# Span attention later in the batch, shorter, with its sums on ScalarE: one change to a perceiver block on one Trainium2 core

## The chip, the core and the metric

The kernel runs on one core of one Trainium2 chip. The core has a matrix engine (TensorE, PE in profiles; PEld is its loading of weights), a vector engine (VectorE, DVE), an activation engine (ScalarE, ACT), a general one (GpSimd, POOL), a queue engine that starts most transfers here (SyncE, SP), and DMA engines. Every engine works through its own list of instructions in order and waits for the others by semaphores. TensorE writes to PSUM, which VectorE and ScalarE read; GpSimd works on SBUF alone here. The metric is the device time of one execution in microseconds (us).

## The reference

Thirty-two sequences of 64 latent rows of width 256 go through three blocks, each with a layer norm before it and a residual addition after it. All values are float32.

```python
x = x + xattn(layernorm(x), ctx, ctx, mask)  # 16 heads of 16; ctx has 1601 rows per sequence
x = x + span_attn(layernorm(x))
x = x + ffn(layernorm(x))                    # gated dense part, and two of eight experts per row
```

The span attention is the part of most interest here. For each head it computes two numbers per row and a distribution over the 64 positions:

```python
span = heads(h @ W_span.T, 2);  value = heads(h @ W_val.T, 16)
mean = sigmoid(span[..., 0]) * 64
soft = softplus(span[..., 1])
scores = -soft * (pos - mean) ** 2
out = softmax(scores) @ value
return merge(out) @ W_out.T
```

## The kernel before

**Cross attention, in halves of a batch.** The loop over `halves` (L696) runs over the 32 sequences ("batches" in the code) and, in each, over c = 0 and 1, eight heads at a time. The 1601 context rows lie in 13 blocks of 124, and these in four groups (`GROUPS`: four blocks, then three times three). One pass of the loop is half n. It has four stretches, g = 0 to 3, numbered 4n + g, and in each the code issues for every engine, in this order: the scores of the *next* half for group g (`scores`, TensorE, into four PSUM banks, and VectorE takes them out with the mask added, L504); projections of the next batch (`project_keys`, `project_values`, TensorE, and ScalarE takes them out, L465 and L482); a subtraction of the maxima of *this* half for one of four pairs of heads (`less_maxima`, L556, on GpSimd in the loop); then the steps that the agenda holds for this stretch (`run`); and one exponential of a pair (`exponentials`, L561, ScalarE).

The maxima over the blocks are gathered in `mrun`, a PSUM tile: `first_maxima` (L517, ScalarE) copies block 0 into it at the end of g = 0, and VectorE takes the further blocks in (`maximum`, L525) between the evictions and after those of g = 3, where the last one writes `mx`. In g = 0 of the next half TensorE turns it (`turned_maxima`, pm, L532), VectorE reduces it (L539), TensorE spreads it over the partitions (pb, L547), and ScalarE copies it out (mb, L551). The first subtraction on GpSimd waits for that.

The products with the values (`values`, pvs, L571) are issued in two parts: r = 0 at the head of a half and r = 1 in its g = 0 after the agenda; they need the exponentials of the half before. Between g = 0's `run` and `first_maxima`, `mrun` is free, and its first row of columns serves the agenda as scratch (`aside`).

All projections, scores and other products of the loop draw their PSUM bank from one ring of six (`mm_bank`).

`project_values(b, u)` handles unit u: two blocks of values (the last unit has one). With c = 0 unit 0 comes in g = 1 and units 1 and 2 in g = 3; with c = 1 unit 3 comes in g = 1, 4 in g = 2, 5 and 6 in g = 3. A "tiled" product is issued in four pieces of 32 columns.

**The agenda.** Two batches make a tile of 128 rows; there are 16. `finish_steps` (VectorE) closes a batch in g = 1 of the second half after it. After the second batch of a tile it puts `span_steps` on the agenda, one stretch later. This is a generator, cut by `yield next(waits)`; each number is the number of stretches until the next step, from `WAITS`, or from `CLOSE` for the last two tiles. Its steps are: output projection of the cross attention, addition, statistics; normalisation; transposes; the product psp and `z`; an exponential of `z`; the value product pval and its copies to `vbd`; the small chain (L279 to L295) that makes `mean` and `soft` on [128, 16] tiles, partly in the scratch; `pos - mean` on GpSimd (L300); the square (ScalarE, L304) and the product with `soft` (GpSimd, L305); the minimum (VectorE, L308) and its subtraction (GpSimd, L309); the exponential over [128, 16, 64] (ScalarE, L311); the sum and its reciprocal (VectorE, L313, L314) and the product with it (GpSimd, L315); transposes (L323); the weighted sum (L333); the output product (L343), addition, statistics and a store of x; normalisation; transposes into `xfT` (L354). `query_steps` prepares the queries of the next tile in the same way.

`spread_of` and `normalised` are the layer norm: statistics on VectorE, a power of -1/2 on GpSimd (L187), and two activations (L193, L194).

**The order is written out by hand.** From L662 to L805 the four compute engines take their instructions in the order of the code. An instruction put ahead of another on the same engine goes first, whether or not its inputs are ready.

**After the loop** comes a tail: the last half without new scores, the steps of the last two tiles, and the dense part of the feed-forward block in between; then the experts.

Of the kernel before, what the change touches and what calls it, by code (L numbers as in the profile page):

```python
# [15 lines left out]
F32 = mybir.dt.float32  # L16
U8 = mybir.dt.uint8
AF = mybir.ActivationFunctionType
ALU = mybir.AluOpType
AX = mybir.AxisListType  # L20
PSUM = bass.MemoryType.PSUM

P = 128
S = 64
D = 256
H = 16
# [6 lines left out]
GROUPS = [(0, 4), (4, 3), (7, 3), (10, 3)]  # L33
BETWEEN = [(), (1, 2, 3), (4, 5, 6), (7, 8, 9), (10, 11, 12)]
LN_EPS = 1e-5
MASKED = -1e30
BIG = 3e38
E, TOPK, PRIME, HASH_OFF = 8, 2, 11, 7919
# [36 lines left out]
def perceiver_kernel(ctx: ExitStack, tc: tile.TileContext, a: dict[str, bass.AP], out: bass.AP):  # L75
    nc = tc.nc
# [6 lines left out]
    const = ctx.enter_context(tc.tile_pool(name="const", bufs=1))  # L83
    work = ctx.enter_context(tc.tile_pool(name="work", bufs=2))
# [79 lines left out]

    neghalf = const.tile([P, 1], F32, name="neghalf")
    nc.gpsimd.memset(neghalf, -0.5)
    own4 = const.tile([P, 2], F32, name="own4")
    nc.vector.tensor_scalar(own4, own, 0.25, None, ALU.mult)

# [6 lines left out]
    def spread_of(src, name: str):  # L176

        stats = work.tile([P, 6], F32, tag="stats", name=f"stats_{name}")
        nc.vector.bn_stats(stats, src)
        mv = work.tile([P, 2], F32, tag="mv", bufs=4, name=f"mv_{name}")  # L180
        nc.vector.bn_aggr(mv, stats)
        neg = work.tile([P, 1], F32, tag="neg", bufs=4, name=f"neg_{name}")
        nc.vector.tensor_scalar(neg, mv[:, 0:1], -1.0, None, ALU.mult)
        ve = work.tile([P, 1], F32, tag="ve", bufs=4, name=f"ve_{name}")
        nc.vector.tensor_scalar(ve, mv[:, 1:2], LN_EPS, None, ALU.add)
        rstd = work.tile([P, 1], F32, tag="rstd", bufs=4, name=f"rstd_{name}")
        nc.gpsimd.tensor_tensor(rstd, ve, neghalf, ALU.pow)  # L187
        return neg, rstd

    def normalised(src, spread, name: str):  # L190
        neg, rstd = spread
        xn = work.tile([P, D], F32, tag="xn", name=f"xn_{name}")
        nc.scalar.activation(xn, src, AF.Identity, bias=neg)  # L193
        nc.scalar.activation(xn, xn, AF.Copy, scale=rstd)  # L194
        return xn

    def transposed(src, name: str):
# [9 lines left out]

    WAITS = (1, 1, 1, 1, 1, 1, 1, 1, 1, 1, 1, 3, 3, 1, 1, 1)  # L210
    CLOSE = (1, 1, 1, 1, 0, 2, 1, 1, 1, 1, 1, 2, 1, 1, 1, 1)

    def span_steps(t: int, oT):
        waits = iter(CLOSE if t >= NTILE - 2 else WAITS)
# [9 lines left out]
        h = normalised(x, spread, f"h{t}")  # L224
        yield next(waits)
        ps = transposed(h, f"h{t}")
# [10 lines left out]
        z = span_pool.tile([P, H, 2], F32, tag="z", name=f"z_{t}")  # L237
# [13 lines left out]
        for b in range(2):  # L251
            for c in range(2):
                for j in range(4):
                    e, i = divmod(j, 2)
# [13 lines left out]
        def small(tag: str):  # L268
            return span_pool.tile([P, H], F32, tag=tag, name=f"{tag}_{t}")
# [1 line left out]


        held = aside(f"held_{t}")
        num, den, rat, atp, acc = (held[:, i * H : (i + 1) * H] for i in range(5))
        s0, s1, z0, z1 = span[:, :, 0], span[:, :, 1], z[:, :, 0], z[:, :, 1]
        mean, soft, rden, at, twice, at2 = (
            small(n) for n in ("mean", "soft", "rden", "at", "twice", "at2")
        )
        nc.vector.tensor_scalar(rat, z1, 2.0, None, ALU.add)  # L279
        nc.vector.tensor_scalar(den, z0, 1.0, None, ALU.add)  # L280
        nc.vector.tensor_scalar(num, s0, 0.0, None, ALU.is_ge)
        nc.vector.reciprocal(rat, rat)
        nc.vector.reciprocal(rden, den)
        nc.vector.tensor_tensor(num, z0, num, ALU.max)
        nc.vector.tensor_tensor(atp, z1, rat, ALU.mult)
        nc.vector.tensor_tensor(at, z1, rat, ALU.mult)
        nc.vector.scalar_tensor_tensor(twice, z1, 2.0, rat, ALU.mult, ALU.mult)
        nc.vector.tensor_tensor(at2, at, atp, ALU.mult)
        nc.vector.scalar_tensor_tensor(mean, num, float(S), rden, ALU.mult, ALU.mult)

        nc.vector.tensor_scalar(acc, at2, 1.0 / 15, None, ALU.mult)
        for n in (13, 11, 9, 7, 5, 3):
            nc.vector.scalar_tensor_tensor(acc, acc, 1.0 / n, at2, ALU.add, ALU.mult)  # L293
        nc.vector.scalar_tensor_tensor(acc, acc, 1.0, twice, ALU.add, ALU.mult)
        nc.vector.scalar_tensor_tensor(soft, s1, 0.0, acc, ALU.max, ALU.add)  # L295
        yield next(waits)
# [1 line left out]
        full = [P, H, S]  # L298
        sc = span_pool.tile(full, F32, tag="sc", name=f"sc_{t}")
# [6 lines left out]
        yield next(waits)  # L306
        least, total = small("least"), small("total")
        nc.vector.tensor_reduce(least, sc, AX.X, ALU.min)  # L308
        nc.gpsimd.tensor_tensor(sc, sc, least[:, :, None].to_broadcast(full), ALU.subtract)  # L309
        yield next(waits)  # L310
        nc.scalar.activation(sc, sc, AF.Exp, scale=-1.0)  # L311
        yield next(waits)
        nc.vector.tensor_reduce(total, sc, AX.X, ALU.add)  # L313
        nc.vector.reciprocal(total, total)  # L314
        nc.gpsimd.tensor_tensor(sc, sc, total[:, :, None].to_broadcast(full), ALU.mult)  # L315
        yield next(waits)
# [2 lines left out]
        for q in range(2):  # L319
            ps = mm_bank(f"psa_{t}_{q}")  # L320
            for i in range(4):
                n = 4 * q + i
# [6 lines left out]
        for c in range(2):  # L329
            for b in range(2):  # L330
                for j in range(4):
                    n = 4 * c + j
# [17 lines left out]
        xn = normalised(x, spread, f"f{t}")  # L350
        yield next(waits)
        ps = transposed(xn, f"f{t}")
        for c in range(2):
            nc.vector.tensor_copy(  # L354
                xfT[:, c, :, t * PER : (t + 1) * PER], ps[:, c].rearrange("p (i r) -> p r i", r=E)
            )

# [51 lines left out]
    def query_steps(t: int):  # L409
        spread = spread_of(xs[t], f"q{t}")  # L410
        yield 1
        xn = normalised(xs[t], spread, f"q{t}")
        yield 1
        ps = transposed(xn, f"q{t}")
        xnT = work.tile([P, 2, P], F32, tag="xnT", name=f"xnT_{t}")
        nc.vector.tensor_copy(xnT, ps)
        yield 1
        pq = mm_bank(f"pq_{t}")
        for c in range(2):
            for i in range(2):  # L420
                nc.tensor.matmul(
                    pq[:, c * P : (c + 1) * P], lhsT=wqT[:, i, c * P : (c + 1) * P],
                    rhs=xnT[:, i, :], start=(i == 0), stop=(i == 1),
                )

        q = work.tile([P, 2, 2, 2, S], F32, tag="qbd", name=f"qbd_{t}")
        for c in range(2):
            for e in range(2):
                nc.scalar.activation(
                    q[:, c, :, e, :], pq[:, c * P : (c + 1) * P].rearrange("p (b q) -> p b q", b=2),  # L430
                    AF.Identity, bias=bq4[:, c, e : e + 1], scale=own4[:, e : e + 1],
                )
        qbd[t] = q
        yield 1

        nc.gpsimd.tensor_tensor(xs[t], xs[t], bo_row, ALU.add)
# [259 lines left out]
    for n, (b, c) in enumerate(halves[:-1]):  # L696
        if c == 0 and b + 1 < B:
            load_context(b + 1)
        if c and b % 2 == 0 and b // 2 + 1 < NTILE:
            agenda[4 * n + 2].append(query_steps(b // 2 + 1))  # L700

        def project(f, *args):
            if b + 1 < B:
                f(b + 1, *args)

        if n:
            values(n - 1, 0)
            exponentials(n - 1, 3)
        for g in range(len(GROUPS)):
            if g == 0:  # L710
                turned = []

                def turn():
                    turned.extend(turned_maxima(n))
                    return turned

                scores(n + 1, g, BETWEEN[g], turn)
                project(project_keys, c, 0)
                m = maxima_along_rows(turned[1])
                less_maxima(n, 0, m, nc.gpsimd)  # L720
                run(4 * n)
                if n:
                    values(n - 1, 1)
                    if c == 0:
                        agenda[4 * n + 1].append(finish_steps(b - 1, 4 * n + 1))
            else:
                scores(n + 1, g, BETWEEN[g])
                project(project_keys, c, g, g == 3)
                if g == 1:
                    project(project_values, 3 * c)  # L730
                elif g == 2 and c:
                    project(project_values, 4)
                elif g == 3:
                    for u in range(5 if c else 1, 7 if c else 3):
                        project(project_values, u, True)
            if g:
                less_maxima(n, g, m, nc.gpsimd)
                run(4 * n + g)
            for u in extra.get(4 * n + g, ()):
                linear_factor(u)  # L740
            if g == 0:
                first_maxima(n + 1)
            else:
                exponentials(n, g - 1)
        for k in BETWEEN[-1]:
            maximum(n + 1, k)
# [176 lines left out]
```

## Time and profile before

| what | value |
|---|---|
| runs shown | 1578.86, 1575.32, 1578.23 us; median 1578.23 |
| profiled execution | 1579.34 us |
| its span, first to last instruction | 1577.4 us |
| mean granted TensorE clock | 0.995 |
| L504 evictions of scores, VectorE | 1024, 567.5 us in all, 580 ns each |
| L525 maxima, VectorE | 704, 483.5 us in all, 687 ns each |
| L556 subtractions, GpSimd | 252, 936.6 us in all, 3735 ns each |
| L561 exponentials of pairs, ScalarE | 256, 403.1 us in all, 1587 ns each |
| L308, L313 minimum and sum, VectorE | 16 each, 1201 and 1210 ns |
| L300, L305, L309, L315, GpSimd | 16 each, 1904 to 1910 ns |
| L311 exponential of span attention, ScalarE | 16, 1067 ns |
| L293 of the small chain, VectorE | 96, 182 ns |
| L187 power, GpSimd | 48, 551 ns |
| L193, L194 normalisation, ScalarE | 48 each, 508 to 520 ns |
| L416 query copy, L354 xfT copies, VectorE | 16 of 414 ns, 32 of 281 ns |

The page lists for each engine the time in which it was busy. Since the engines overlap, busy times do not add up to the span; the chain of waits, followed back from the last instruction, tells which engine's work the end depended on. A timeline row reads: start, duration, engine, line, operation, output <- inputs, shapes, count, and in brackets how long the engine stood idle before it and what released it. Rows of the same kind in succession are merged, so a count of 2 covers two instructions. In the chain an instruction counts only from the moment the one before it let go, so its share may be shorter than its duration.

### The profile page before, as it was taken

The page shows a single profiled execution, that of the slowest core. Times are in us where ns is not written, and L with a number is a line of the kernel's source. Part 1 is how long each engine was busy: PE and PEld are TensorE (multiplying, and loading weights), DVE is VectorE, ACT ScalarE, POOL GpSimd, SP SyncE. Part 2 cuts the span into 40 slices and gives each one's busy share as a digit, 9 for nine tenths or more (in the row PEclk, how much of TensorE's full clock was granted, in tenths as well). Part 3 has the DMA queues.
Part 4 walks back from the last instruction along what each step waited for, and adds up shares of the span by engine and source line. Part 5 has one row for each costly group of instructions (what it writes and reads, how often), then busy time and mean ns, then how long its engine had stood idle before and what let it go on. Part 6 is the DMA issues. An engine that isn't in the chain of part 4 may idle for free.

```text
span 1577.4 us, 62735 instructions
## 1 busy us (share of the span) xinstructions
PE 1518.3 (96%) x28600; PEld 1090.8 (69%) x28600; DVE 1259.5 (80%) x2700; ACT 897.1 (57%) x1229; POOL 1121.6 (71%) x424
## 2 busy tenths in 40 slices
PE   8999999999999999999999999999999999988899
PEld 5676776777767676676767676676767676754587
DVE  4888889898888888898889988898888988884200
ACT  2565656566565656656666656565655656555311
POOL 1777877878687877788786977788786878761610
PEclk9999999999999999999999999999999999999999
DMA  5111111111111111111111111111111111004100
GB/s 166 54 42 44 36 38 38 45 51 44 51 44 44 39 41 35 35 51 44 52 44 51 36 43 38 38 38 45 51 44 52 44 37 41 7 2 154 57 27 27
DMA packets 52072, 73.78 MB, mean 47 GB/s; under 512 B 3812, under 2 KB 51040, under 8 KB 51680
## 3 DMA queue, kind: packets, MB, share of 16 engines
q1 hardware_dynamic: 50992, 69.00, 15.3%
q8 instruction: 224, 3.67, 1.0%
q10 hardware_dynamic: 816, 0.79, 0.2%
q14 instruction: 40, 0.33, 0.1%
HBM read 65.57 MB, written 4.19 MB: 44 GB/s over the span
## 4 chain that ended last, share of the span: by engine, by line
PE 60%; DVE 36%; issue 2%; ACT 1%; DMA 1%; POOL 1%; ACTq 0%; SPq 0%; DVEq 0%; POOLq 0%
DVE prob L504 14%; PE pv L450 13%; PE pk L450 13%; DVE mrun L525 12%; PE pvs L571 9%; PE psc L495 9%; PE py L853 4%; PE u L600 3%; PE pm L532 2%; PE ph L835 2%; PE pb L547 1%; DVE total L313 1%; DVE least L308 1%; DVE mrun L293 1%; PE po L343 1%
## 5 line engine op out<-in xcount | busy, mean ns | idle before, releaser
L556 POOL TENSOR_TENSOR prob<-prob,mb 124x1664 f32<-124x1664 f32 x252 | 936.6, 3735 | 275.2 <-ACT mb L551 188.2
L504 DVE TENSOR_TENSOR prob<-psc,madd 124x384 f32<-124x384 f32 (+1 forms) x1024 | 567.5, 580 | 152.2 <-PE psc L495 152.2
L525 DVE TENSOR_TENSOR mrun<-prob,mrun 124x512 f32<-124x512 f32 x704 | 483.5, 687 | 3.9
L561 ACT ACTIVATE prob<-prob 124x1664 f32<-124x1664 f32 x256 | 403.1, 1587 | 26.0 <-POOL prob L556 23.0
L450 PE MATMUL pk<-ct,wkT_sb 128*32 128x361 f32 (+2 forms) x1768 | 404.8, 499 | 9.5 <-DMA wkT_sb<-in_wkT 5.4
L450 PE MATMUL pv<-wvT_sb,ct 128*32 128x256 f32 (+3 forms) x4268 | 385.8, 379 | 0.0
L450 PEld LDWEIGHTS pv<-wvT_sb,ct 128*32 128x32 f32 (+3 forms) x4268 | 258.6, 123 | 128.8 <-issue 16.3
L495 PE MATMUL psc<-qbd,kT 32*124 32x128 f32 x6656 | 288.2, 285 | 24.1 <-DVE prob L504 21.5
L465 ACT ACTIVATE kT<-pk,cols 128x372 f32<-128x372 f32 (+2 forms) x256 | 152.1, 594 | 239.4 <-PE pk L450 239.1
L495 PEld LDWEIGHTS psc<-qbd,kT 32*124 32x124 f32 x6656 | 226.2, 181 | 89.3 <-DVE prob L504 47.0
L482 ACT COPY v<-pv 124x512 f32<-124x512 f32 (+1 forms) x224 | 124.9, 558 | 211.0 <-PE pv L450 210.8
L450 PEld LDWEIGHTS pk<-ct,wkT_sb 128*32 128x32 f32 (+1 forms) x1768 | 158.6, 145 | 119.3 <-issue 51.5
L571 PE MATMUL pvs<-prob,v 124*17 124x64 f32 x13312 | 213.2, 220 | 2.3 <-issue 2.2
L571 PEld LDWEIGHTS pvs<-prob,v 124*17 124x17 f32 x13312 | 195.8, 98 | 22.5 <-issue 13.8
L517 ACT COPY mrun<-prob 124x512 f32<-124x512 f32 x64 | 38.5, 602 | 59.5 <-DVE soft L295 56.3
L855 DVE SCALAR_TENSOR_TENSOR ot<-py,prob 128x256 f32<-128x256 f32 x16 | 6.8, 425 | 75.7 <-PE py L853 66.1
L600 PE MATMUL u<-xfT,sw_sb 128*128 128x512 f32 x128 | 60.2, 620 | 1.3 <-ACT vbd L262 0.9
L547 PEld LDWEIGHTS pb<-cst,mc 128*124 128x124 f32 x256 | 29.2, 136 | 36.5 <-DVE mc L539 29.4
L532 PE MATMUL pm<-cst,mx 124*128 124x124 f32 x256 | 40.7, 282 | 8.3 <-DVE mx L525 8.2
L525 DVE TENSOR_TENSOR mx<-prob,mrun 124x512 f32<-124x512 f32 x64 | 43.9, 686 | 2.2
L842 ACT ACTIVATE hT<-ph,cols 128x256 f32<-128x256 f32 x32 | 13.4, 471 | 56.3 <-PE ph L835 56.3
L600 PEld LDWEIGHTS u<-xfT,sw_sb 128*128 128x128 f32 x128 | 24.5, 198 | 29.9 <-issue 25.3
(126 smaller groups left out, 1143.4 us busy)
## 6 DMA issues: line engine op xcount, KB each, us to landing
ct<-in_ctxT SPq DMA_DIRECT2D x64, 372.0 KB, 3.2
ct<-in_ctxT SPq DMA_DIRECT2D x32, 496.0 KB, 3.6
ct<-in_ctxT SPq DMA_DIRECT2D x32, 361.0 KB, 3.1
w<-in_w SPq DMA_DIRECT2D x16, 256.0 KB, 5.9
x<-in_x SPq DMA_DIRECT2D x16, 128.0 KB, 2.2
x_kept<-x SPq DMA_DIRECT2D x16, 128.0 KB, 2.8
prob<-x_kept SPq DMA_DIRECT2D x8, 256.0 KB, 5.4
out<-ot SPq DMA_DIRECT2D x16, 128.0 KB, 1.9
```

Of the source, the lines that this page charges most:

```text
L450: nc.tensor.matmul(out[at:end], lhsT=lhsT[:, at:end], rhs=rhs, start=start, stop=stop, **(dict(tile_position=(0, at)) if tiled else {}),)
L465: nc.scalar.activation(kTs[c][:, k0 : k0 + kn], ps[:, :kn], AF.Identity, bias=cols[:, B_K + c : B_K + c + 1])
L482: nc.scalar.copy(vs[b % 2][:kn, 2 * u : 2 * u + n, :, :DK], ps[:kn, : n * D].rearrange("p (n h d) -> p n h d", n=n, d=DK),)
L495: nc.tensor.matmul(ps[:CHUNK, k * P : (k + 1) * P], lhsT=kTs[c][32 * j : 32 * j + 32, at : at + CHUNK], rhs=qbd[b // 2][32 * j : 32 * j + ...
L504: nc.vector.tensor_tensor(pair_of(n, j)[:, c0 : c0 + nb, :].rearrange("p k (e q) -> p k e q", e=2), ps[:CHUNK, : nb * P].rearrange("p (k e ...
L525: nc.vector.tensor_tensor(dst, block_of(n, k), run, ALU.max)
L532: nc.tensor.transpose(ps[:, j * CHUNK : (j + 1) * CHUNK], m[:CHUNK, j, :], ident[:CHUNK, :CHUNK])
L556: engine.tensor_tensor(sj, sj, m[:CHUNK, j, None, :].to_broadcast([CHUNK, NKC, P]), ALU.subtract)
L561: nc.scalar.activation(pair_of(n, j), pair_of(n, j), AF.Exp)
L571: nc.tensor.matmul(pvs[32 * j : 32 * j + DK + 1, c, :, r, :], lhsT=v[:kn, k, 8 * c + h, :], rhs=pair_of(n, h // 2)[:kn, k, (h % 2) * S : ( ...
L600: nc.tensor.matmul(ps, lhsT=w[:, c, hc * P : (hc + 1) * P], rhs=xfT[:, c, :, slot], start=(c == 0), stop=(c == 1),)
L853: nc.tensor.matmul(py, lhsT=x, rhs=w, start=(n == 0), stop=(n == len(terms) - 1))
```

## The change

1. `project_values` for c = 0: unit 1 moves from g = 3 (tiled) to g = 2 (whole). c = 1 stays as it was.
2. `WAITS` gets one step more and a longer wait before pval; every later step of span attention, up to `xfT`, comes four stretches later than before. `CLOSE` gets the additional step; pval there comes two stretches later and the other steps stay.
3. The small chain has 15 instructions in place of 20. The two additions and the two reciprocals are joined, and the series for the logarithm has five fitted coefficients in place of seven of 1/n.
4. The subtraction of the minimum on GpSimd, the one exponential and the sum on VectorE go. In their place ScalarE runs 16 exponentials of 64 columns, one per head, each with its minimum as the bias and its sum as a second output, eight in one step and eight in the next.
5. Layer norm: two small operations move from VectorE to GpSimd, where there are now three, and one activation with bias and scale takes the place of two. The copies of the transposed queries and of `xfT` move from VectorE to ScalarE.

```diff
-        nc.vector.tensor_scalar(neg, mv[:, 0:1], -1.0, None, ALU.mult)
-        nc.vector.tensor_scalar(ve, mv[:, 1:2], LN_EPS, None, ALU.add)
-        nc.gpsimd.tensor_tensor(rstd, ve, neghalf, ALU.pow)
+        nc.gpsimd.tensor_scalar(rstd, mv[:, 1:2], LN_EPS, None, ALU.add)
+        nc.gpsimd.tensor_tensor(rstd, rstd, neghalf, ALU.pow)
+        nc.gpsimd.tensor_scalar(neg, mv[:, 0:1], rstd, -1.0, ALU.mult, ALU.mult)
...
-        nc.scalar.activation(xn, src, AF.Identity, bias=neg)
-        nc.scalar.activation(xn, xn, AF.Copy, scale=rstd)
+        nc.scalar.activation(xn, src, AF.Identity, bias=neg, scale=rstd)
...
-    WAITS = (1, 1, 1, 1, 1, 1, 1, 1, 1, 1, 1, 3, 3, 1, 1, 1)
-    CLOSE = (1, 1, 1, 1, 0, 2, 1, 1, 1, 1, 1, 2, 1, 1, 1, 1)
+    WAITS = (1, 1, 1, 1, 5, 1, 1, 1, 1, 1, 1, 1, 2, 3, 1, 1, 1)
+    CLOSE = (1, 1, 1, 1, 2, 0, 1, 1, 1, 1, 0, 1, 2, 1, 1, 1, 1)
...
+        nc.vector.tensor_tensor(over, z, one_two, ALU.add)
+        nc.vector.tensor_scalar(ge, s0, 0.0, None, ALU.is_ge)
+        nc.vector.reciprocal(over, over)
+        nc.vector.tensor_tensor(num, z0, ge, ALU.max)
+        nc.vector.tensor_tensor(atp, z1, over[:, :, 1], ALU.mult)
+        nc.vector.scalar_tensor_tensor(twice, z1, 2.0, over[:, :, 1], ALU.mult, ALU.mult)
+        nc.vector.scalar_tensor_tensor(mean, num, float(S), over[:, :, 0], ALU.mult, ALU.mult)
+        nc.vector.scalar_tensor_tensor(at2, twice, 0.5, atp, ALU.mult, ALU.mult)
+        nc.vector.tensor_scalar(acc, at2, ATANH[-1], None, ALU.mult)
+        for a in ATANH[-2::-1]:
+            nc.vector.scalar_tensor_tensor(acc, acc, a, at2, ALU.add, ALU.mult)
...
         nc.vector.tensor_reduce(least, sc, AX.X, ALU.min)
-        nc.gpsimd.tensor_tensor(sc, sc, least[:, :, None].to_broadcast(full), ALU.subtract)
-        yield next(waits)
-        nc.scalar.activation(sc, sc, AF.Exp, scale=-1.0)
-        yield next(waits)
-        nc.vector.tensor_reduce(total, sc, AX.X, ALU.add)
+        yield next(waits)
+        for part in range(2):
+            for h in range(part * H // 2, (part + 1) * H // 2):
+                nc.scalar.activation(
+                    sc[:, h, :], sc[:, h, :], AF.Exp, bias=least[:, h : h + 1], scale=-1.0,
+                    accum_out=total[:, h : h + 1],
+                )
+            yield next(waits)
...
-            nc.vector.tensor_copy(
+            nc.scalar.copy(
                 xfT[:, c, :, t * PER : (t + 1) * PER], ps[:, c].rearrange("p (i r) -> p r i", r=E)
             )
...
-        nc.vector.tensor_copy(xnT, ps)
+        nc.scalar.copy(xnT, ps)
...
                 if g == 1:
                     project(project_values, 3 * c)
-                elif g == 2 and c:
-                    project(project_values, 4)
-                elif g == 3:
-                    for u in range(5 if c else 1, 7 if c else 3):
+                elif g == 2:
+                    project(project_values, 3 * c + 1)
+                else:
+                    for u in (5, 6) if c else (2,):
                         project(project_values, u, True)
```

## The prediction, made before the changed kernel was run

> **What bounds the kernel now.** I read the page first: busy shares, then the chain that ended last.
>
> ```profile
> PE 1518.3 (96%) x28600; PEld 1090.8 (69%) x28600; DVE 1259.5 (80%) x2700; ACT 897.1 (57%) x1229; POOL 1121.6 (71%) x424
> ...
> PE 60%; DVE 36%; issue 2%; ACT 1%; DMA 1%; POOL 1%; ACTq 0%; SPq 0%; DVEq 0%; POOLq 0%
> ```
>
> TensorE is nearly always busy, yet 36% of the chain is VectorE: the bound alternates. To see where, I cut the span at the first transpose of the column maxima (pm, L532), one per half-batch. Four halves make a tile; I call them A and B (c = 0 and 1 of the even batch), C and D (of the odd one), and A2 the stretch g = 2 of A. The table of windows gives busy times for one such tile, A to D downwards:
>
> ```profile
> core 0: us, PE busy (x) PEld busy (x) DVE busy (x) ACT busy (x) POOL busy (x), PEclk, DMA share, GB/s
> 732.53:754.81 22.28, 21.79 (x468) 15.46 (x465) 18.50 (x38) 12.82 (x18) 15.68 (x6) 1.00 0.04 11
> 754.81:777.10 22.29, 22.29 (x460) 16.79 (x457) 18.93 (x42) 14.58 (x23) 15.88 (x6) 1.00 0.31 88
> 777.10:800.15 23.05, 21.56 (x434) 15.34 (x431) 22.17 (x56) 14.03 (x20) 19.47 (x8) 1.00 0.01 3
> 800.15:820.06 19.91, 19.77 (x412) 14.06 (x413) 17.28 (x31) 12.26 (x15) 17.95 (x6) 1.00 0.29 75
> ```
>
> B is TensorE throughout. C, which holds the small chain of L279 to L295, is VectorE (22.2 of 23.05). In A and D VectorE sets the end: it waits about 2 to 3 us after each pm, for the scores behind pk, pb and pvs, and then runs without a gap to the next pm. Over the 13 tiles from 205.1 to 1345.8 us the means are A 22.3, B 22.5, C 23.05, D 19.9, together 87.7.
>
> TensorE's own need comes from the spacing in the chain of waits: pm 0.57, pk 1.67 + 1.45 + 1.45 + 1.35, pb 0.44, pvs 1.58 + 1.46, psc 3 x 0.86 + 1.08, and 1.73 for each two blocks of values. That is 18.8 us with c = 0 and 19.7 with c = 1, plus the steps of span attention. For B the sum is 22.21, and its shortest instances last 22.21: the method holds.
>
> **Part 1, values one unit a stretch.** Only c = 0 changes: unit 1 goes from g = 3 to g = 2. A unit takes 1.73 us tiled (32 matmuls) or whole (8 matmuls), so TensorE's sum stays. It shortens what stands in front of the next pm, but in A VectorE's own run ends there as well. I count nothing; cover gone, it is at most the 0.3 us and 0.6 us waits for psc banks.
>
> **Part 2, the schedule.** The value product moves B3 to C3, the small chain C0 to D0, the scores' POOL and ScalarE steps C1-C3 to D1-D3, the exponentials D0 to A0 and A1, the division A2, the eight transposes A0 to B0, the weighted sum A3 to B3, the output product, addition and norm B0-B2 to C0-C2. The x_kept store moves four stretches on SP; it is read only at the tail, and x has four buffers, so nothing waits.
>
> *C* loses chain and minimum on VectorE and becomes TensorE's: 18.8 + output product 0.86 + query transposes and product 1.3 + transposes 0.22 + value product 0.87 = 22.05; with the 0.2 that B averages over its sum, **22.25, minus 0.8**. VectorE would need about 21.
>
> *B* gives up output product, two transposes and value product (1.95) and takes 0.87 + 0.45: 22.5 - 0.6 = **21.8, minus 0.65**.
>
> *D* takes the chain and the minimum. The chain has 15 instructions for 20. The old one ran 780.57 to 784.53, 3.96 us; five fewer at 0.2, the two reciprocals become one of 32 columns (0.27 to about 0.38): 3.05. VectorE starts it at 3.14 after pm, ends it at 6.2, and three rounds of evictions and maxima of 3.65 bring it to the minimum at 17.2. But the minimum needs GpSimd, whose order is copied here from C:
>
> ```profile
> 780.68 7.38 POOL L556 TENSOR_TENSOR prob<-prob,mb 124x1664 f32<-124x1664 f32 x2 [6.28 <-DVE xnT L416]
> 788.02 1.90 POOL L300 TENSOR_TENSOR sc<-cst,mean 128x1024 f32<-128x1024 f32 x1
> 789.88 3.74 POOL L556 TENSOR_TENSOR prob<-prob,mb 124x1664 f32<-124x1664 f32 x1
> 793.57 0.74 POOL L436 TENSOR_TENSOR x<-x,bo_row 128x256 f32<-128x256 f32 x1
> 794.26 1.91 POOL L305 TENSOR_TENSOR sc<-sc,soft 128x1024 f32<-128x1024 f32 x1
> ```
>
> The product with soft ends 19.07 us after C's pm; in D only L436 is gone, so 18.4. The chain of waits shows what comes between the minimum and the next pm:
>
> ```profile
> 796.84 1.11 DVE least L308
> ...
> 800.15 0.30 PE pm L532
> ```
>
> Three maxima stand between; by the timeline the minimum starts at 796.75, so 3.4 us from its start. D becomes 18.4 + 3.4 = **21.8, plus 1.9**. The work saved in the chain buys nothing here: GpSimd is late next.
>
> **Part 3, the exponentials.** They replace one subtraction of 1.91 on GpSimd, one exponential of 1.07 and one sum of 1.21 on VectorE by 16 activations of 64 columns. The order on ScalarE in A0 is now:
>
> ```profile
> 735.43 0.58 ACT L551 COPY mb<-pb 124x512 f32<-124x512 f32 x1
> 735.89 1.09 ACT L325 COPY aT<-psa 128x512 f32<-128x512 f32 x2
> 736.85 0.62 ACT L517 COPY mrun<-prob 124x512 f32<-124x512 f32 x1
> ```
>
> Eight exponentials take the place of the aT copies, ahead of first_maxima (L517). VectorE's first maximum of A1 waits for that copy. With a spacing p, the copy is ready at 4.0 + 8p after pm. The maximum stands at 739.93 now, 7.4 after pm; without the psa transposes at about 6.4. From it to the next pm VectorE takes 14.88 (to 754.81); less 0.14 for L183 and L185, plus 0.26 for the reciprocal (L314), 15.0. So A = max(6.4, 4.0 + 8p) + 15.0.
>
> p is in no row. The Trainium skill (ScalarE: Activation LUTs, What ACT_TABLE_LOAD costs) gives an activation 186 ns + 0.833 ns per element, 93 more for a pointer operand, and 93 of overlap: 0.24 us here, with no price for the sum; A would be 21.4. The nearest row speaks of more: the 128x32 exponential (L246) takes 232 ns without a pointer, and its successor starts 130 ns after it. If the read of each sum is a second small instruction of that sort, p is 0.24 + 0.13 to 0.24 + 0.23 = 0.37 to 0.47; with no overlap at all 0.33 + 0.23 = 0.56. I take 0.40: **A = 22.2, minus 0.1**. The second eight (A1) delay kT and v of A2 by 3.2; TensorE needs those banks some 14 us after pm and has 1.5 to 2 us to spare in A, so I count nothing.
>
> **Part 4, norms.** VectorE loses 0.14 per norm and the xnT (0.33) and xfT (0.4) copies, in C and B, where TensorE bounds: nothing. ScalarE gives one 0.51 of two. GpSimd's 0.55 power gets two neighbours, some 1.1 us more. The skill (GPSIMD Engine Reference, Engine selection) advises against small elementwise work there, and the rows agree (551 ns against 144 to 154); but GpSimd idles 5.3 us at the start of B and 5 in A, so by rule plus 1.1 a norm on the path, by these rows nothing. Cover gone, a late fourth subtraction holds ScalarE in the next half by up to 0.6.
>
> **Sum.** A steady tile: -0.1 - 0.65 - 0.8 + 1.9 = +0.35, 13 times +4.5. First tile: C without chain -2, B -0.9, D +1.9: -1.1. Last: A, B and C together -0.4. Loop +3. In the tail nothing hides the exponentials:
>
> ```profile
> 1425.81 1.05 ACT sc L311
> ...
> 1426.88 1.23 DVE total L313
> ...
> 1430.49 1.97 PE psa L323 x8
> ```
>
> From 1425.81 to the reciprocal's end at 1428.40 becomes 16 x 0.4 + 0.25 = 6.65: +4.05. For the last tile the stretch from the minimum's end (1459.37) to the reciprocal's (1463.98), 4.6, becomes 6.65: +2.05. TensorE idles longer and its clock row is already at 0.76 and 0.75 there: +0.5. Tail +6.6. Together **+9.6 us**. The profiled execution took 1579.34 (span 1577.4), which lies 1.1 above the median of 1578.23; 1588 on the median.
>
> **Rivals.** *Cheap sums.* p = 0.24: the copy is in time, A drops to 21.4, 14 x 0.8 = 11 us; the tail costs 1 instead of 6.6: about 1571, faster. The change of sign lies at p = 0.33. For it: ScalarE does overlap (four L429 of 457 ns end in 1.51). Against it: an extra result has to be written. 0.15.
> *Dear sums.* p = 0.5 to 0.56: A 23 to 23.5, tail +10 to +12: 1602 to 1612. 0.22.
> *Relief everywhere.* If GpSimd's product came early enough in D (chain alone: 20.6) and the copy were no gate, a tile would be 22.25 + 20.6 + 21.4 + 21.8 = 86.05, 1.65 less: with the tail about 1556. Against it: four GpSimd rows that can't be reordered. 0.05.
> *No effect*, gains and gates level at p near 0.33: 1578. 0.12.
> The forecast has the rest, 0.46. A measurement here tells about 0.2% (3 us) from no change. Slower 0.46 + 0.22 = 0.68, same 0.12, faster 0.15 + 0.05 = 0.20. The likeliest case's own range, p from 0.37 to 0.47, is 1583 to 1598; for 8 in 10 it reaches from the cheap to the dear sums, 1570 to 1612.
>
> **What would show it.** Distances between pm transposes: D near 21.8 with VectorE idle before the minimum on L305; C near 22.2 with TensorE full; A showing L525 waiting for L517. A spacing of the 64-column exponentials under 0.3 us makes the forecast wrong, and so does a D under 21.

## The result, and the profile after

| | before | after |
|---|---|---|
| median of four runs each, same chip, us | 1578.55 (1575.32 to 1579.92) | 1590.92 (1589.00 to 1592.15) |
| ratio, 95% interval | | 1.0074 (1.0058 to 1.0089) |
| profiled execution, its span, us | 1579.34, 1577.4 | 1589.0, 1586.9 |
| mean granted TensorE clock | 0.995 | 0.986 |
| loop, to the last pm, us of the span | 1413.3 | 1420.3 |
| tail, after it, us | 164.1 | 166.7 |

The change made the kernel slower by 12.4 us, where 9.6 were forecast. The busy shares and the chain of waits of the changed kernel:

```profile
PE 1508.6 (95%) x27856; PEld 1099.6 (69%) x27856; DVE 1209.5 (76%) x2460; ACT 954.2 (60%) x1725; POOL 1117.8 (70%) x506
...
PE 59%; DVE 23%; POOL 11%; ACT 5%; issue 2%; DMA 0%; ACTq 0%; DVEq 0%; POOLq 0%
```

VectorE lost 50 us of work and a third of its share of the chain. What it lost went to GpSimd (from 1% of the chain to 11%) and ScalarE (1% to 5%). The windows cut at pm show where. Four rows are one tile, A to D; the fifth is the A that follows:

```profile
core 0: us, PE busy (x) PEld busy (x) DVE busy (x) ACT busy (x) POOL busy (x), PEclk, DMA share, GB/s
730.83:752.19 21.36, 20.36 (x401) 14.80 (x401) 18.30 (x38) 16.71 (x46) 17.72 (x9) 1.00 0.01 3
752.19:773.77 21.58, 21.58 (x459) 16.22 (x459) 16.90 (x33) 13.85 (x21) 16.10 (x8) 1.00 0.28 76
773.77:796.03 22.26, 22.26 (x449) 16.94 (x445) 18.54 (x37) 14.75 (x24) 16.61 (x8) 1.00 0.06 17
796.03:817.93 21.90, 19.80 (x415) 14.09 (x413) 20.02 (x46) 11.85 (x15) 18.35 (x6) 1.00 0.28 78
817.93:840.91 22.98, 21.98 (x401) 15.42 (x401) 18.30 (x38) 16.83 (x46) 17.73 (x9) 0.93 0.01 2
```

B and C are TensorE without a gap. D has 2.1 us in which TensorE does nothing. The two A do the same work, yet one is 1.62 us longer, at a granted clock of 0.93 in place of 1.00. Over the steady halves (8 to 59):

| mean length, us | A | B | C | D |
|---|---|---|---|---|
| before | 22.32 | 22.46 | 23.05 | 19.91 |
| forecast | 22.2 | 21.8 | 22.25 | 21.8 |
| after | 22.30 | 21.86 | 22.27 | 21.89 |

VectorE's timeline at the end of D shows the gate (start, duration, engine, line, operation; in brackets how long it had been idle and what released it):

```profile
812.41 0.69 DVE L526 TENSOR_TENSOR mrun<-prob,mrun 124x512 f32<-124x512 f32 x1
814.49 1.22 DVE L306 TENSOR_REDUCE least<-sc 128x16 f32<-128x1024 f32 x1 [1.40 <-POOL sc L303]
815.63 1.42 DVE L526 TENSOR_TENSOR mrun<-prob,mrun 124x512 f32<-124x512 f32 x2
817.08 0.69 DVE L526 TENSOR_TENSOR mx<-prob,mrun 124x512 f32<-124x512 f32 x1
```

The minimum stands ahead of the last three maxima in VectorE's order, and waits 1.40 us for GpSimd's product with soft. Pm waits for the last maximum, and TensorE has nothing else to do. TensorE's timeline at the same place:

```profile
814.65 1.15 PE L496 MATMUL psc<-qbd,kT 32*124 32x128 f32 x32
817.91 0.61 PE L533 MATMUL pm<-cst,mx 124*128 124x124 f32 x4 [2.10 <-DVE mx L526]
818.36 3.13 PE L451 MATMUL pk<-ct,wkT_sb 128*128 128x496 f32 x4
```

Two things are to be seen. The pause is 2.10 us in one piece (1.92 in most tiles). And the keys' product after it takes 3.13 us for four matmuls, against 1.83 at the start of the other A. The granted clock there reads 0.50 for 3.41 us. Such a stretch follows D's pause in 9 of 14 tiles; in the loop of the kernel before there is none. Each of these nine A is longer than 21.36, by 1.17 to 1.64 us; together they are 13.8 us longer, more than the whole loss.

The list of TensorE's waits (in all, times, longest, in us), two rows of before:

```profile
PE psc L495 <- DVE prob L504: 21.5, 44, 0.6
PE pm L532 <- DVE mx L525: 8.2, 15, 3.6
```

and the first two of after:

```profile
PE pm L533 <- DVE mx L526: 46.3, 32, 3.6
PE psa L324 <- POOL sc L316: 9.3, 2, 5.6
```

Before, TensorE's waiting for VectorE lay in 44 pieces of half a microsecond; now it stands in front of pm.

### The profile page after: what moved, and what is told of

The parts are those of the page before. It is cut to its first block, busy times and chain, and to the rows that moved or that the text cites. A ratio compares the mean times of both kernels' runs of the same rounds, so it can differ in the third digit from the quotient of the medians.

```text
span 1586.9 us, 61590 instructions
## 1 busy us (share of the span) xinstructions
PE 1508.6 (95%) x27856; PEld 1099.6 (69%) x27856; DVE 1209.5 (76%) x2460; ACT 954.2 (60%) x1725; POOL 1117.8 (70%) x506
## 4 chain that ended last, share of the span: by engine, by line
PE 59%; DVE 23%; POOL 11%; ACT 5%; issue 2%; DMA 0%; ACTq 0%; DVEq 0%; POOLq 0%
PE pk L451 15%; PE pv L451 12%; DVE mrun L526 9%; PE psc L496 8%; POOL prob L557 7%; DVE prob L505 7%; PE pvs L572 6%; PE py L854 3%; ACT sc L310 3%; PE u L601 2%; PE pm L533 2%; POOL sc L303 2%; PE ph L836 2%; POOL sc L298 2%; DVE mx L526 1%
## 5 line engine op out<-in xcount | busy, mean ns | idle before, releaser
L451 PE MATMUL pk<-ct,wkT_sb 128*32 128x361 f32 (+2 forms) x1768 | 416.1, 506 | 7.1 <-DMA wkT_sb<-in_wkT 5.5
L451 PE MATMUL pv<-wvT_sb,ct 128*124 128x256 f32 x3524 | 390.9, 379 | 0.0
L451 PEld LDWEIGHTS pv<-wvT_sb,ct 128*124 128x124 f32 x3524 | 273.5, 132 | 119.8 <-issue 16.8
L496 PE MATMUL psc<-qbd,kT 32*124 32x128 f32 x6656 | 267.1, 284 | 3.9 <-issue 2.3
L496 PEld LDWEIGHTS psc<-qbd,kT 32*124 32x124 f32 x6656 | 214.0, 181 | 57.2 <-DVE mrun L526 14.4
L310 ACT ACTIVATE sc<-sc,least 128x64 f32<-128x64 f32 x256 | 85.3, 338 | 0.8 <-DVE least L306 0.8
L533 PEld LDWEIGHTS pm<-cst,mx 124*128 124x128 f32 x256 | 27.0, 143 | 55.9 <-issue 33.4
L548 PEld LDWEIGHTS pb<-cst,mc 128*124 128x124 f32 x256 | 32.5, 145 | 40.8 <-DVE mc L540 23.6
L316 POOL TENSOR_TENSOR sc<-sc,total 128x1024 f32<-128x1024 f32 x16 | 30.5, 1903 | 27.9 <-DVE total L315 27.5
```

What stands on the lines that cost most here:

```text
L310: nc.scalar.activation(sc[:, h, :], sc[:, h, :], AF.Exp, bias=least[:, h : h + 1], scale=-1.0, accum_out=total[:, h : h + 1],)
L451: nc.tensor.matmul(out[at:end], lhsT=lhsT[:, at:end], rhs=rhs, start=start, stop=stop, **(dict(tile_position=(0, at)) if tiled else {}),)
L496: nc.tensor.matmul(ps[:CHUNK, k * P : (k + 1) * P], lhsT=kTs[c][32 * j : 32 * j + 32, at : at + CHUNK], rhs=qbd[b // 2][32 * j : 32 * j + ...
L533: nc.tensor.transpose(ps[:, j * CHUNK : (j + 1) * CHUNK], m[:CHUNK, j, :], ident[:CHUNK, :CHUNK])
```

## The experiments

The first four kernels put these questions: does GpSimd's gate in D carry the loss, are the exponentials to blame for a part, and do the chain and the values, which the prediction put at nothing or nearly so, matter? In all that follows, "the changed kernel" is the one that the prediction is about, and each time is a median, with its ratio to the kernel before on the same chip.

**The minimum one stretch later** (A0 instead of D3; exponentials A1 and A2, total in A3).

```diff
-    WAITS = (1, 1, 1, 1, 5, 1, 1, 1, 1, 1, 1, 1, 2, 3, 1, 1, 1)
+    WAITS = (1, 1, 1, 1, 5, 1, 1, 1, 2, 1, 1, 1, 1, 3, 1, 1, 1)
```

> The minimum comes one stretch later (A0), the exponentials in A1 and A2, sum and division in A3; everything else is as in the changed kernel. Theory (in D VectorE waits for GpSimd's product before the minimum, TensorE then pauses about 2 us, and in half of the tiles its clock is halved for 3.4 us after the pause): D falls from 21.9 to 20.6 to 20.8, no clock row under 1.0 is left in the loop, A goes to 21.2 to 21.4, the time to about 1560, under that of before. Rival 1 (the 16 exponentials are what costs): they still run, so 1585 to 1595. Rival 2 (VectorE's own work in D, with the chain in it, is what costs): the minimum only moves from D to A, so D minus 1.2 and A plus 1.2, the time unchanged near 1590.

Measured: 1559.80 us, ratio 0.9864 (0.9847 to 0.9882). One stretch of delay for one step, two numbers in a list of waits, moves the time by 31 us. The windows of a tile from A to D (columns as above):

```profile
371.80:393.90 22.10, 20.66 (x405) 14.74 (x401) 19.44 (x38) 16.22 (x46) 19.06 (x9) 1.00 0.04 12
393.90:415.48 21.58, 21.58 (x463) 16.22 (x459) 17.06 (x33) 13.92 (x22) 16.73 (x8) 1.00 0.28 76
415.48:437.36 21.88, 21.88 (x449) 16.67 (x445) 18.50 (x36) 14.37 (x24) 16.60 (x8) 1.00 0.06 18
437.36:457.26 19.90, 19.76 (x417) 14.02 (x413) 18.76 (x44) 12.23 (x15) 16.36 (x6) 1.00 0.27 73
```

D is back at 19.9, B and C keep their gains, and the clock is whole everywhere in the loop. D fell further than expected (19.9, not 20.6 to 20.8) and A less (22.1, not 21.2 to 21.4), so the expected 1560 came out because the two misses cancel. A's TensorE timeline has a new wait:

```profile
375.66 1.63 PE L572 MATMUL pvs<-prob,v 124*17 124x64 f32 x100 [0.93 <-ACT prob L562]
```

Because D is shorter, its fourth subtraction on GpSimd ends after pm, and the values' product waits 0.93 us for that pair's exponential. What comes late next is GpSimd again. The 31 us are not the gate's alone: the move also takes the minimum's own 1.2 us out of D, into A0, where it starts 3.1 us after pm, in time in which VectorE waited 2.35 us for scores in the changed kernel. The run with the squares, below, takes away the gate and leaves the minimum in D.

**The old exponential in the changed schedule**: subtraction on GpSimd behind the minimum in D, one exponential of 1024 columns in A0, sum on VectorE in A2.

```diff
         nc.vector.tensor_reduce(least, sc, AX.X, ALU.min)
+        nc.gpsimd.tensor_tensor(sc, sc, least[:, :, None].to_broadcast(full), ALU.subtract)
         yield next(waits)
-        for part in range(2):
...
-            yield next(waits)
+        nc.scalar.activation(sc, sc, AF.Exp, scale=-1.0)
+        yield next(waits)
+        yield next(waits)
+        nc.vector.tensor_reduce(total, sc, AX.X, ALU.add)
```

> The changed kernel with the old form of the exponentials: subtraction on GpSimd behind the minimum in D3, one exponential in A0, sum on VectorE in A2. Theory: D stays at 21.9 and the halved clock stays; A without its 0.4 us wait for the copy but with 1.2 us more on VectorE goes from 21.4 to about 22.1 (without the clock's share); the tail is 3 to 4 us shorter; together 1591 to 1601. Rival 1 (the exponentials cost): back to 1575 to 1582. Rival 2 (VectorE's work costs): plus 1.2 x 14, about 1605.

Measured: 1609.64 us, ratio 1.0181 (1.0159 to 1.0202), above all three expectations. The tail is 4.4 us shorter (162.2), as a tail without the sixteen exponentials should be; the loop is 24.7 longer. Two of its windows, an A and its B:

```profile
831.60:855.36 23.76, 21.72 (x400) 14.96 (x400) 19.40 (x39) 12.83 (x15) 19.59 (x10) 0.93 0.01 2
855.36:879.61 24.25, 23.63 (x458) 17.21 (x458) 16.92 (x33) 14.91 (x21) 16.14 (x8) 0.93 0.26 70
```

The sum puts 1.2 us back on VectorE in A, so that TensorE's pause before the pm at A's end grows from 1.0 to 2.02 us, and now B has a clock of 0.93 too: 12 of 14 B have a stretch of 0.50, beside 7 of the A. The halved clock is not all of it: an A at the full clock lasts 22.07, against 21.36. The sixteen exponentials are therefore not what cost time in the loop; without them it is worse. They cost in the tail.

**The old small chain of 20 instructions in its new place.**

```diff
-        nc.vector.tensor_tensor(over, z, one_two, ALU.add)
...
-        for a in ATANH[-2::-1]:
+        nc.vector.tensor_scalar(rat, z1, 2.0, None, ALU.add)
+        nc.vector.tensor_scalar(den, z0, 1.0, None, ALU.add)
...
+        nc.vector.reciprocal(rat, rat)
+        nc.vector.reciprocal(rden, den)
...
+        for n in (13, 11, 9, 7, 5, 3):
```

> The changed kernel with the small chain of before (20 instructions, 0.9 us longer). Theory: in D VectorE waits 1.4 us for GpSimd before the minimum, so the longer chain is hidden: D stays at 21.9, time 1590 to 1593. Rival 2 (VectorE's work in D sets its end): D plus 0.9, time plus 13, about 1604.

Measured: 1575.15 us (eight runs), ratio 0.9977 (0.9962 to 0.9991). Every expectation missed: five instructions more make the changed kernel 15.8 us *faster*. D is as long as it was (21.85), since the minimum still waits for GpSimd, for 0.26 us, where the D shown above waits 1.40 and most D of the changed kernel 1.21:

```profile
459.38 1.22 DVE L311 TENSOR_REDUCE least<-sc 128x16 f32<-128x1024 f32 x1 [0.26 <-POOL sc L308]
```

What changed is how TensorE's pause lies, by its timeline:

```profile
449.25 0.48 PE L501 MATMUL psc<-qbd,kT 32*124 32x128 f32 x4
450.18 0.92 PE L501 MATMUL psc<-qbd,kT 32*124 32x128 f32 x20 [0.45 <-DVE prob L510]
451.24 1.21 PE L456 MATMUL pk<-ct,wkT_sb 128*128 128x372 f32 x3
...
462.79 0.61 PE L538 MATMUL pm<-cst,mx 124*128 124x124 f32 x4 [0.97 <-DVE mx L531]
463.25 1.83 PE L456 MATMUL pk<-ct,wkT_sb 128*128 128x496 f32 x4
```

VectorE, busy with the longer chain, frees the banks for g = 2 later: the keys' product behind these scores starts 1.99 us after them (451.24 - 449.25), against 0.92 in the changed kernel. By so much less is left to wait before pm: 0.97 us. After that the keys' product takes 1.83, no tile of the loop has a clock of 0.50, and every A lasts 21.35. D does the same work on TensorE in the same time, so the total pause is about the same; in two pieces (1.07 us by the spacing, and 0.97) it costs 15.8 us less. That made a new theory: an unbroken pause of about 2 us lets the clock drop, and the drop is what makes the change slow. (The two pieces are some 11 us apart, and no run sets two close together. Whether the pause has to be unbroken, or only long enough within a few us, is not shown.)

**Unit 1 of the values back in g = 3**, tiled, as before the change.

```diff
-                elif g == 2:
-                    project(project_values, 3 * c + 1)
-                else:
-                    for u in (5, 6) if c else (2,):
+                elif g == 2 and c:
+                    project(project_values, 4)
+                elif g == 3:
+                    for u in range(5 if c else 1, 7 if c else 3):
```

> The changed kernel with unit 1 of the values back in g = 3, tiled. As predicted (it counts for nothing, at most for 0.3 to 0.6 us waits of TensorE for score banks): 1591 to 1605. Rival (it is a large part of the gain in A and C): without it TensorE waits in C2 and A2 for VectorE's evictions and then has 1.7 us more ahead of the next pm; A plus 0.7 and C plus 1.2 give 1610 to 1620. Third: the early unit is itself what costs: back towards 1580.

Measured: 1618.19 us, ratio 1.0239 (1.0212 to 1.0266). So part 1 is worth 27 us inside the changed kernel, and the rival's 1610 to 1620 came out. Its C lasts 23.24 on average and 23.02 at best, A 21.79 at best and 22.43 on average, with six stretches of halved clock in the loop. The list of TensorE's waits has two entries that are 0.6 us or nothing in the changed kernel:

```profile
PE psc L496 <- DVE prob L505: 6.8, 19, 0.6
PE psc L496 <- ACT kT L466: 5.6, 14, 0.8
```

With unit 1 gone from g = 2 there is less in front of the scores of g = 3, and TensorE arrives before ScalarE has taken out the keys and VectorE has freed the banks. Three pauses of 1.2 to 2.1 us in its B the profile doesn't attribute; they stay open.

**A second group**, with the clock theory stated. First, **sixteen activations with Square** on ScalarE, with the (negated) mean as bias, take the place of GpSimd's pos - mean and of the whole square. This frees GpSimd ahead of the product with soft and moves nothing else.

```diff
-        nc.gpsimd.tensor_tensor(
-            sc, pos[:, None, :].to_broadcast(full), mean[:, :, None].to_broadcast(full), ALU.subtract
-        )
-        yield next(waits)
-        nc.scalar.activation(sc, sc, AF.Square)
+        for part in range(2):
+            for h in range(part * H // 2, (part + 1) * H // 2):
+                nc.scalar.activation(sc[:, h, :], pos, AF.Square, bias=mean[:, h : h + 1])
+            if part == 0:
+                yield next(waits)
```

> The changed kernel, but the subtraction pos - mean on GpSimd (1.9 us in D1) and the square behind it are 16 activations with the mean as bias on ScalarE, eight in D1 and eight in D2. Nothing else moves; the minimum stays in D3. Theory (GpSimd's order sets the end of D): the product with soft ends near 16.6 after pm in place of 18.4, VectorE reaches the minimum at 17.3 and sets the end: D 20.6 to 20.8 in place of 21.9, TensorE's pause under 1 us, no halved clock in the loop, A 21.35; time 1558 to 1566. Rival (GpSimd's order in D is not the gate, or 16 more activations cost as much): D stays at 21.9 and the time at 1588 to 1595.

Measured: 1563.47 us, ratio 0.9900 (0.9877 to 0.9922), as the theory had it. The windows of a D and of the A behind it:

```profile
437.02:457.73 20.71, 20.15 (x417) 14.32 (x413) 20.01 (x46) 14.77 (x30) 16.49 (x5) 1.00 0.29 78
457.73:479.07 21.34, 20.35 (x400) 14.79 (x400) 18.28 (x38) 16.72 (x46) 17.72 (x9) 1.00 0.02 6
```

D falls to 20.71, near the 20.6 that the prediction gave for the chain alone without the gate; the minimum no longer waits, and starts 17.3 us after pm. The pause falls to 0.43, no clock of 0.50 is left in the loop, and A lasts 21.35. With the same minimum in the same place, the gate was GpSimd's product, as forecast. The tail grows by 6.2 us, since there nothing hides the activations.

**The norms back on VectorE** (the two small operations, the two activations, and the copies of xnT and xfT):

```diff
-        nc.gpsimd.tensor_scalar(rstd, mv[:, 1:2], LN_EPS, None, ALU.add)
-        nc.gpsimd.tensor_scalar(neg, mv[:, 0:1], rstd, -1.0, ALU.mult, ALU.mult)
+        nc.vector.tensor_scalar(neg, mv[:, 0:1], -1.0, None, ALU.mult)
+        nc.vector.tensor_scalar(ve, mv[:, 1:2], LN_EPS, None, ALU.add)
...
-        nc.scalar.copy(xnT, ps)
+        nc.vector.tensor_copy(xnT, ps)
```

> The changed kernel with the norms' small operations and the copies of the queries and of xfT back on VectorE, and two activations per norm. As predicted (they lie in C and B, where TensorE bounds, and 0.14 us in A): 1590 to 1595. Rival 1 (taking them off VectorE is worth several tenths of a us per tile in A and C): 1597 to 1605. Rival 2 (three small operations on GpSimd are a cost of the change): 1580 to 1588.

Measured: 1597.07 us, ratio 1.0106 (1.0078 to 1.0134): 6 us worse than the changed kernel. A without a halved clock lasts 21.62, 0.26 more, and C 22.02 at best, 0.14 more, with one halved stretch more in the loop. The intervals of the two ratios overlap (1.0058 to 1.0089, and 1.0078 to 1.0134), so the size is rough; the sum of these parts, 14 x 0.26 + 13 x 0.14 + 1.6 = 7 us, speaks for it. The first rival came out, at its lower edge: part 4 is a small gain.

**The minimum later, and the old exponential for the last two tiles alone**, to see whether the sixteen exponentials are what makes the tail long:

```diff
+        closing = t >= NTILE - 2
+        if closing:
+            nc.gpsimd.tensor_tensor(sc, sc, least[:, :, None].to_broadcast(full), ALU.subtract)
...
+            if closing and part == 0:
+                nc.scalar.activation(sc, sc, AF.Exp, scale=-1.0)
...
+        if closing:
+            nc.vector.tensor_reduce(total, sc, AX.X, ALU.add)
```

> The minimum one stretch later as in the first experiment, and for the last two tiles, whose steps lie in the tail, the old form of the exponentials. If the 16 exponentials lengthen the tail (2.7 and 1.1 us on the chain before the transposes), 1555 to 1557 against 1559.8. Rival (the tail's end hangs on other work): 1559 to 1561.

Measured: 1555.49 us, ratio 0.9847 (0.9825 to 0.9869); its tail is 162.5 us, against 168.5 with the minimum later alone. The sixteen exponentials do lengthen the tail.

**All of it together**: minimum later, old exponential at the end, squares on ScalarE.

> The last one with the squares on ScalarE too, so that both of GpSimd's gates are off. In the first experiment's A TensorE waits 0.9 us for the fourth exponential of a pair, which is late since GpSimd ends D's fourth subtraction 2.2 us after the next pm; with 1.9 us less on GpSimd this goes: A from 22.1 to 21.2 to 21.5, D stays 19.9, time 1545 to 1551. Rival (A is bound by VectorE or by the second wait, for the second exponential): A stays above 21.8, 1553 to 1558.

Measured: 1547.35 us, ratio 0.9797 (0.9773 to 0.9821), the fastest of all. The windows of a tile:

```profile
709.60:730.49 20.89, 20.38 (x404) 14.63 (x400) 19.44 (x38) 16.26 (x46) 17.54 (x9) 1.00 0.04 15
730.49:752.07 21.58, 21.58 (x462) 16.22 (x458) 17.06 (x33) 13.91 (x22) 16.81 (x8) 1.00 0.28 76
752.07:774.19 22.12, 22.12 (x448) 16.91 (x444) 18.49 (x36) 14.60 (x24) 16.57 (x8) 1.00 0.06 17
774.19:794.40 20.21, 20.19 (x414) 14.34 (x412) 18.83 (x44) 14.56 (x30) 15.97 (x5) 1.00 0.28 72
```

B, C and D are TensorE without a gap, and A lacks 0.5 us of it. (The sum was as expected, the parts not quite: A is 0.3 us shorter than the range given, D 0.3 longer than 19.9.) Most of what is left to gain in the loop lies in TensorE's own work.

**The pause filled.** The old chain had shown the clock theory only by a side road, so it got a run of its own: the changed kernel, with three products of 256 columns into the bank of pm ahead of the pm that ends D. The transposes overwrite them. This adds work to TensorE and takes none away.

```diff
         ps = mm_bank("pm")
+        for _ in range(3 if n % 4 == 0 and n else 0):
+            nc.tensor.matmul(
+                ps[:, :D], lhsT=wvT[:, 0, :P], rhs=wvT[:, 1, :], start=True, stop=True
+            )
         for j in range(4):
```

> The changed kernel with three products of 256 columns ahead of the transposes that end D, about 1.3 us of work for TensorE whose result is overwritten; it adds work and takes none away, and it fills the pause of 1.9 us in front of pm. Theory (it is the unbroken pause that gets the clock halved, as the run with the longer chain suggests): D stays at 21.9, the pause falls to about 0.6, no clock row under 1.0 in the loop, every A 21.36; time 1574 to 1578, with more work. Rival (the longer chain helped in another way, or pauses have nothing to do with the clock): the halved rows stay, 1590 to 1593.

Measured: 1574.66 us (20 runs), ratio 0.9976 (0.9967 to 0.9984). TensorE's timeline at the end of a D:

```profile
462.92 1.56 PE L533 MATMUL pm<-wvT_sb 128*128 128x256 f32 x6
464.84 0.64 PE L537 MATMUL pm<-cst,mx 124*128 124x124 f32 x4 [0.35 <-DVE mx L526]
465.32 1.83 PE L451 MATMUL pk<-ct,wkT_sb 128*128 128x496 f32 x4
```

and the windows of this D and of the A behind it:

```profile
443.02:464.84 21.82, 21.32 (x423) 15.07 (x419) 19.95 (x46) 12.27 (x15) 18.24 (x6) 1.00 0.28 77
464.84:486.22 21.38, 20.38 (x401) 14.82 (x401) 18.38 (x38) 16.71 (x46) 17.85 (x9) 1.00 0.01 3
```

D is as long as in the changed kernel, and every A now lasts 21.38. Products whose result nobody reads made the kernel 16.3 us faster than the changed one; 13.8 of it are the nine long A. That the pause brings the halved clock, and the halved clock the loss, is shown by this run.

## Why the prediction was right, and where only its sum was

Direction and size came out. The step that carried the loss did too: in D the minimum comes behind GpSimd's product. Freeing GpSimd (27 us) shows it, and moving the minimum (31 us) agrees. But that the sum came out above zero is luck: without the halved clock in A, which the prediction does not have, its own account gives no change, as is worked out under A.

*D, 18.4 + 3.4 = 21.8.* Measured: the minimum starts 18.48 after pm, the half lasts 21.89. "The work saved in the chain buys nothing here" held for D's length, and said too little: the saved 0.9 us gathered TensorE's pause into one piece, and with that brought the halved clock; putting the work back gained 15.8 us.

*C, 22.25, and B, 21.8.* 22.27 and 21.86; sums over TensorE's list hold where TensorE has no gap. (Two sums are rounded loosely: B is 22.46 - 0.63, and the first tile adds up to -1.0, not -1.1. Neither matters.)

*A, 22.2.* Its mean of 22.30 agrees for a reason that was not foreseen. The term that was mis-sized is p, taken as 0.40. On ScalarE's timeline one exponential and the read of its sum are two rows:

```profile
734.16 0.36 ACT L310 ACTIVATE sc<-sc,least 128x64 f32<-128x64 f32 x1
734.41 0.20 ACT L310 ACTIVATION_READ_ACCUMULATOR sc<-sc,least 128x1 f32 x1
734.51 0.34 ACT L310 ACTIVATE sc<-sc,least 128x64 f32<-128x64 f32 x1
...
736.83 0.58 ACT L518 COPY mrun<-prob 124x512 f32<-124x512 f32 x1
```

and VectorE's timeline has the first maximum behind that copy:

```profile
737.45 0.70 DVE L526 TENSOR_TENSOR mrun<-prob,mrun 124x512 f32<-124x512 f32 x1 [0.44 <-ACT mrun L518]
```

The pairs follow one another every 0.333 us. That is the 0.24 estimated from the Trainium skill (ScalarE: Activation LUTs, What ACT_TABLE_LOAD costs) and 0.09 for the read, below the 0.13 to 0.23 that I allowed it. The gate is there but cuts little: 0.44 us, and A lasts 21.36 (the forecast's formula gives 21.7 with this p; from the copy's end to the next pm it is 14.7 us, not 15.0). By the prediction's own account p = 0.33 is where the sign turns, and without the clock it would have been so: 1590.9 - 13.8 = 1577.1, no change that can be told (the run with the pause filled measured 1574.7). The 0.94 between 21.36 and 22.30 is the halved clock, of which the prediction has no word for the loop; it counted the idle time in D as a loss of its own length alone.

*Part 1 at nothing, part 4 at nothing.* Both were costed against the kernel before. In the changed one they are worth 27 and about 6 us. C at 22.25 has TensorE without a gap, and that is only so if the scores' banks and keys are in time, which unit 1 in g = 2 provides: the cover of one part was made by the other. In part 4 the two added operations on GpSimd take 0.22 and 0.27 us, 0.5 and not 1.1 a norm.

*Loop +3, tail +6.6.* Measured +6.9 and +2.6 in the two profiled executions, 9.5 together (12.4 between the medians); the total agrees since the errors cancel. In the loop the thirteen steady tiles gave +7.4 where 4.5 stood, all four halves being within 0.1 of their forecasts. All that lies ahead of them gave -2.9 (-1.1 forecast). The last tile's A to C gave +2.4 (-0.4 forecast), nearly all of it in C: that C has no projections, so the newly placed pval and output product (2.1 us) stand in front of its scores for g = 1, together with a product of the feed-forward block (2.0) that stood there before, and leave VectorE idle for 1.96. In the tail the chain of waits of after reads

```profile
1432.84 3.37 ACT sc L310 x21
...
1436.63 1.52 ACT sc L310 x9
1438.15 0.02 issue
1438.17 0.27 DVE total L315
...
1438.57 1.91 POOL sc L316
...
1440.53 1.97 PE psa L324 x8
```

5.3 us for the sixteen and 5.6 to the reciprocal's end, not 6.65. The first transposes come 3.1 us later in the tail than before (+4.05 forecast), those of the last tile 1.4 later again (+2.05). Of these 4.5 us, 1.9 came back before the end, where I had put down +0.5 for the clock: one of TensorE's stretches of 0.50 there is 3.41 us long in place of 6.83, which is worth at most 1.7. That this is the reason was not tried.

*Rivals.* "No effect", with its p near 0.33, would have been the outcome but for the clock. Cheap sums came nearest in its price (p = 0.333, its turning point) and failed in its time. Relief everywhere was right in what it asked for and is what the changed schedule gives once GpSimd is free: 1563.5 with the squares, 1547.4 with the rest. It had 0.05; its objection, "four GpSimd rows that can't be reordered", looked only at the order and not at moving one of the four.

## What to carry to other kernels

When a step is moved to a stretch with a shorter list on the bounding engine, place it by when its *last* input is ready there, and look at what stands behind it in its engine's order: here one stretch more is worth 31 us. A part that costs nothing against the old schedule can be what the new one rests on; cost each part inside the changed kernel. And look at the length of TensorE's longest single pause, not only at the sum: in this kernel two pauses of 1 us were cheaper than one of 2 us, and even products that nobody reads paid.

## What the runs showed of the hardware

In the changed kernel, pauses of TensorE of 1.91 to 2.15 us at the end of D were followed by a granted clock of 0.50 for 3.41 us in 9 of 14 cases; with the old exponential, pauses of 2.02 us at the end of A were in 12 of 13. Pauses of 0.8 to 1.67 us in front of pm (end of A in the changed kernel, end of D with the old chain) never were. Each halved stretch made its A 1.2 to 1.6 us longer in the changed kernel.

The starts lie on a grid: 289.68, 378.43, 467.18 and 555.92 us are 26 steps of 3.413 apart. The grid also tells which pauses escape. Lay it through the halved stretches of four traces (the changed kernel, the old exponential, unit 1 back, the norms back). They have 69 pauses of 1.83 to 2.16 us in front of pm. The 43 that began within the first 1.62 us of a step were all followed by the halved clock; the 26 that began 1.85 us or more into it never were. So 9 of 14 is how the pauses happened to fall. Two of the unattributed pauses with unit 1 back do not fit (one of 2.13 us, begun 1.46 us into a step, was not followed; one of 1.22 us was), so what exactly is counted stays open.

The Trainium skill (TensorE: Matmul & The Clock Gate, Part 1: The HAM clock gate) has that window, free-running, of 3413 ns; its rule under HAM oscillation, no idle gap of more than about 3.4 us, is too lenient here, and the measurement decides.

An activation with a second output for its sum shows as two rows, 338 and 191 ns for 64 columns, which overlap to 0.333 us a pair.
